# Eight more leaf operands, another leaf order and a searched instruction order in a conditioned block by Strassen products

## The chip, the cores and the metric

The kernel runs on one core of one Trainium2 chip. The metric is the device time in microseconds, median of three runs. The engines are TensorE (PE, with its weight loads as PEld), VectorE (DVE), ScalarE (ACT), GpSimd (POOL) and SyncE (SP, which issues nearly all DMAs). Each works through its own queue in order and waits for the others by semaphores.

## The reference

`x` is (2, 2048, 512) in float32, `cond` (2, 512). The result is `x` after two residual steps:

```python
emb = silu(cond) @ ada_w + ada_b              # six rows of 512 per batch
norm = ln(x) * (1 + scale_msa) + shift_msa
h = gelu(norm @ ssm_w1 + ssm_b1)              # 512 -> 512, exact gelu
x = x + gate_msa * (h @ ssm_w2 + ssm_b2)      # 512 -> 512
norm2 = ln(x) * (1 + scale_mlp) + shift_mlp
hf = gelu(norm2 @ ff_w1 + ff_b1)              # 512 -> 1024, tanh gelu
out = x + gate_mlp * (hf @ ff_w2 + ff_b2)     # 1024 -> 512
```

## The kernel before, in words

**Tiling.** The 4096 rows are cut into 8 blocks of 512 (`TB`); blocks 0 to 3 belong to the first batch row, 4 to 7 to the second (`PER_B` = 4). All matrix products are float32, and a product is issued as two matmul records and two weight loads (two passes).

**Products with seven instead of eight.** Every large product is a 2 x 2 block product done with seven products P1 to P7 of sums of quarters (Strassen in Winograd's form). `first` and `second` (L420, L430) form the sums of the operands, with adds on DVE or POOL; the partial results are gathered in PSUM banks and added out by DVE or copied by ACT. In the ff stage this is done twice over: each of the seven outer products is split into seven inner ones, here called leaves.

**Stages.** First come the modulation rows, then for the eight blocks `ssm1` and `ssm2` in alternation with the norms. Then the ff stage runs four times, `s` = 0 to 3, each for two blocks: `ff1(s)`, then `ff2(s, 0)` and `ff2(s, 1)`.

**`ff1` (L1024).** Seven outer products in the order `OUTER`, each with seven leaves in the order `CARRIED` (L445: P1, P5, P6, P2, P7, P3, P4). A leaf is two products of 256 columns. Two outer products overlap: product n begins at step 7n and does a leaf on every second step (L1099 to L1104). So the seventh (n = 6) shares its first three leaves' time with the sixth, and its last four run alone; in the same way the first product's first leaves run alone. P1, P6, P7 and P4 of one outer product write bank y (one after the other onto the same sums), P2 writes x, P5 and P3 write v (`BANK`, L782). After P1, ACT copies bank y to x; after each other leaf, DVE adds its bank to `hidden`. A leaf that writes a bank must wait until the previous reader of that bank is done. After P4 of some outer products, ACT does the gelus of a finished quarter.

**`ff2` (L1114).** Per block seven outer products of 1024 by 512 by 512 quarters; six of them are split into leaves (128 columns, two products a leaf). The seventh, P6, exists in two forms. With `"P6" in wops` (L1149) it too is split into leaves (`sixth`, L1211): P1, P5, P6 and P7 go through bank 7, ACT copies them to `more`, POOL adds, DVE adds `more` into the bank of P1, and P2, P4 and P3 go into that bank directly. Otherwise `plain_sixth` (L1204) runs eight products of 256 columns straight into it. The weights' leaf operands for P6 are formed by `fw2_sixth` (L934): four sums. Before, it is called for the first batch row at `s` = 1 (L1437), so blocks 0 and 1 take the plain form and blocks 2 to 7 the form by leaves.

**The order of the work.** All instructions are first collected as `Op`s with planned costs (`Plan`, L21). TensorE's order is the order in the program. For the others, `order` (L88) works out how late each may be done, back from the planned start of each TensorE instruction; `simulate` (L111) then goes through time and lets every engine take the most urgent op that is ready. An op with engines "vg" goes to DVE or POOL, whichever takes it. SP's DMA issues are put in order in the same way, with a model of one pipe of 370 bytes per ns. The order found is issued as it stands; on the chip only semaphores hold it. `plan.anchor` (L1394) is the first op of `ssm1(0)`.

Of the kernel before, what the change touches and what calls it, by code (L numbers as in the profile page):

```python
# [1 line left out]

# [12 lines left out]


class Op:
    __slots__ = ("n", "engs", "fn", "cost", "lat", "shared", "size", "lead", "care", "after", "done", "sooner", "deps", "succ", "late", "on", "start", "end", "note")


class Plan:  # L21
# [5 lines left out]


    HOP = 70.0
    ISSUE, FLIGHT, LANDING, RATE, BACKLOG = 640.0, 1300.0, 700.0, 370.0, 4000.0  # L30
    NEAR, SPARE = 30000.0, 1500.0
    RATED, LANDED = 0.5, 4000.0
    LITTLE = 1 << 15
    LANES = 8
    AHEAD, SLACK = 2500.0, 150.0

    def __init__(self, nc):
        self.nc = nc
# [47 lines left out]
        return op  # L86

    def order(self):  # L88
        ops = self.ops
        for op in ops:  # L90
            if op.engs == "p":
                op.deps = {d for d in op.deps if ops[d].engs != "p"}
            for d in op.deps:
                ops[d].succ.append(op.n)
        t, due = 0.0, {}
        for op in ops:
            if op.engs == "p":
                due[op.n] = t
                t += op.cost["p"]
        for _ in range(2):  # L100
            for op in reversed(ops):
                late = due.get(op.n, 1e9)
                for s in op.succ:
                    late = min(late, ops[s].late - (1 + op.care) * (self.HOP + min(op.lat.values()) + op.size / self.RATE))
                op.late = late - op.sooner
            self.simulate()
            wait = ops[self.anchor].start - due[self.anchor]
            due = {n: t + wait for n, t in due.items()}
        return sorted(ops, key=lambda op: (op.start, op.n))

    def simulate(self):  # L111
        ops, hop = self.ops, self.HOP
        left, ready = [len(op.deps) for op in ops], [0.0] * len(ops)
        free = dict.fromkeys("pvags", 0.0)
        self.lock, pipe, holder = 0.0, 0.0, None
        tensor = [op for op in ops if op.engs == "p"]
        at, pools, found = 0, {e: [] for e in "vags"}, {}
        lanes = [0.0] * self.LANES

        def enter(op):  # L120
# [31 lines left out]
        count = len(ops)  # L152
        while count:
# [12 lines left out]
            if op.size > self.LITTLE:  # L166
                pipe = max(start + self.FLIGHT, pipe) + op.size / self.RATE * (1 + self.RATED * op.care)
                op.end = pipe + self.LANDING + self.LANDED * op.care
                found.pop("a", None), found.pop("s", None)
            else:  # L170
                op.end = start + op.lat[e]
                if op.size and e == "s":
                    op.end = max(op.end, pipe + self.LANDING)
            if op.size:
                lanes = lanes[1:] + [op.end]
                found.pop("a", None), found.pop("s", None)
            if e in op.shared:
# [10 lines left out]
            count -= 1  # L188
# [10 lines left out]
def kernel(  # L199
# [824 lines left out]
    def ff1(s):  # L1024
# [28 lines left out]
        QUAD = {"P2": "11", "P5": "22", "P6": "12", "P7": "22", "P3": "12", "P4": "21"}  # L1053

        def leaf(n, j):
            p, f = OUTER[n], CARRIED[j]
            bank = {"y": Y_AT[n], "x": X_AT[n % 2], "v": V_AT[n % 2]}
            t = pair(bank[BANK[f]])
            src = cut(inner[n][f], "p a (c q) -> p c a q", q=G)
            half, at = divmod(FW1_AT[f], 4)  # L1060
            for h in range(2):
                mm(t[:, h, :], slot[n][half][:, at, h * P : (h + 1) * P], src, f in ("P1", "P5") and h == 0, f in ("P2", "P3", "P4"))
            if f == "P1":
                copy(pair(bank["x"]), t)
# [352 lines left out]
    for i in range(1, NBLK):  # L1417
# [8 lines left out]
            norm2(i)  # L1426
        if i == 4:
            ff = weight_fw2(0, 1)
        if i + 1 == PER_B:
            w2_ops = weight2(1, 1)  # L1430
            quarter_row(1)
            w2_leaves[0] = second_leaves(w2_ops)
        if not last:
            hid[i + 2] = ssm1(i + 2, tok[i + 2], w1_ops, second_head(i + 1, hid[i + 1]))
    for s in range(NBLK // 2):
        if s == 1:
            fw2_sixth(*ff)  # L1437
        if 2 * s == PER_B:
            ff = weight_fw2_loaded(1)
            fw2_sixth(*ff)  # L1440
# [58 lines left out]
```

## Time and profile before

| | us |
|---|---|
| median of three runs (566.42 to 566.55) | 566.46 |
| the profiled execution | 566.59 |
| its span, first to last instruction | 564.8 |
| TensorE busy in the span | 557.8 |
| DVE / POOL / ACT busy | 483.1 / 379.0 / 266.0 |
| from P4 of ff1(0)'s last product to that of ff1(1) | 87.32 |
| the same, ff1(1) to ff1(2), and ff1(2) to ff1(3) | 86.66, 86.57 |

The granted TensorE clock is at full speed in every slice. A PE row's busy time overlaps that of the next matmul, so the spacing of matmuls is read from counts in a stretch, and a stall from the idle time of the weight loads (PEld) or from the time between two starts. All adds by DVE and POOL have line L256, all plain matmuls L294, ACT's copies L283 and its activations L274, DMA issues L316: they are told apart by their tiles. `hidden` is the ff hidden state and the ssm hidden state, `turned` the transposed normed rows, `ring` weights and sums of ff1's leaves (and `more`), `fw` the second ff weight and its sums, `near` and `far` operand sums of ff2 and scratch of the norms, `rows` the residual, `marks` statistics.

### The profile page before, as it was taken

What the parts mean: (1) busy time and instruction counts of PE and PEld (TensorE: products, weight loads), DVE (VectorE), ACT (ScalarE), POOL (GpSimd) and SP (SyncE); (2) the same over time, 40 slices, a digit from 0 to 9 for tenths busy, and PEclk for the clock granted to TensorE, in tenths of its full rate; (3) what the DMA queues carried; (4) which work ended last, traced back from release to release, by engine and by line L of the source; (5) the groups of instructions that cost most, each with busy time, mean ns of one, the idle gap of its engine ahead of it and who ended that gap; (6) DMA issues with size and microseconds to landing.
All of it is one profiled execution on the core that took longest, in us unless ns stands there. A gap on an engine that the chain in (4) does not pass through costs nothing.

```text
span 564.8 us, 10322 instructions
## 1 busy us (share of the span) xinstructions
PE 557.8 (99%) x3553; PEld 506.3 (90%) x3553; DVE 483.1 (86%) x918; ACT 266.0 (47%) x534; POOL 379.0 (67%) x514
## 2 busy tenths in 40 slices
PE   8999999999999999999999999999999999999997
PEld 4888889888898988889999889999889999888997
DVE  5696978888879989898989899999999888789776
ACT  3473856674888845557102347212366122336120
POOL 2887638979826687995547866776776784446660
PEclk9999999999999999999999999999999999999999
DMA  8953799989799879895047899078956041820022
GB/s 315 398 221 87 233 343 308 316 240 320 223 268 369 257 271 273 273 323 185 4 147 255 302 286 332 18 204 282 321 172 198 2 151 46 272 95 28 1 75 74
DMA packets 53057, 119.85 MB, mean 212 GB/s; under 512 B 5473, under 2 KB 10509, under 8 KB 51470
## 3 DMA queue, kind: packets, MB, share of 16 engines
q1 hardware_dynamic: 51842, 118.66, 63.9%
q8 instruction: 28, 0.46, 0.3%
q10 hardware_dynamic: 1164, 0.55, 0.3%
q14 instruction: 23, 0.19, 0.1%
HBM read 77.63 MB, written 40.51 MB: 209 GB/s over the span
## 4 chain that ended last, share of the span: by engine, by line
PE 94%; DVE 3%; DMA 1%; issue 1%; POOL 0%; SPq 0%; DVEq 0%
PE bank L294 94%; DMA fw<-in_L_cond_ada_w_dram 1%; DVE hidden L256 1%; DVE near L256 0%; DVE marks L522 0%; PE bank L304 0%; POOL hidden L256 0%; POOL near L256 0%; SPq L316 0%; DVE rows L256 0%; DVE ring L256 0%; DVE fw L256 0%; DVE far L591 0%; DVE turned L656 0%; DVE marks L523 0%
## 5 line engine op out<-in xcount | busy, mean ns | idle before, releaser
L294 PE MATMUL bank<-turned,ring 128*128 128x256 f32 x896 | 208.7, 380 | 0.2 <-DVE turned L656 0.2
L294 PEld LDWEIGHTS bank<-turned,ring 128*128 128x128 f32 x896 | 167.6, 190 | 22.9 <-DVE turned L656 0.5
L256 DVE TENSOR_TENSOR hidden<-bank,hidden 128x512 f32<-128x512 f32 (+1 forms) x171 | 125.2, 755 | 28.0 <-PE bank L294 24.8
L294 PE MATMUL bank<-near,hidden 128*128 128x256 f32 (+1 forms) x470 | 95.3, 350 | 0.3 <-DVE rows L256 0.2
L294 PEld LDWEIGHTS bank<-near,hidden 128*128 128x128 f32 x470 | 82.1, 190 | 10.0 <-DVE rows L256 0.6
L294 PE MATMUL bank<-fw,hidden 128*128 128x128 f32 x640 | 90.4, 275 | 0.0
L256 DVE TENSOR_TENSOR rows<-bank,rows 128x128 f32<-128x128 f32 (+3 forms) x154 | 78.8, 554 | 11.4 <-PE bank L294 10.9
L294 PE MATMUL bank<-ring 128*128 128x256 f32 x336 | 82.4, 381 | 0.5 <-DVE hidden L256 0.5
L294 PEld LDWEIGHTS bank<-fw,hidden 128*128 128x128 f32 x640 | 81.2, 192 | 0.4
L283 ACT COPY bank<-bank 128x512 f32<-128x512 f32 (+2 forms) x88 | 37.3, 425 | 83.3 <-PE bank L294 82.2
L256 POOL TENSOR_TENSOR turned<-turned 128x512 f32<-128x512 f32 (+1 forms) x56 | 63.1, 1139 | 16.7 <-ACT turned L274 9.4
L294 PEld LDWEIGHTS bank<-ring 128*128 128x128 f32 x336 | 63.2, 190 | 11.2 <-issue 1.7
L294 PE MATMUL bank<-fw,far 128*128 128x128 f32 (+2 forms) x644 | 67.6, 278 | 0.7 <-DMA fw<-in_L_cond_ada_w_dram 0.7
L294 PEld LDWEIGHTS bank<-fw,far 128*128 128x128 f32 (+1 forms) x644 | 60.9, 167 | 2.7 <-issue 1.7
L274 ACT ACTIVATE hidden<-hidden,cols 128x512 f32<-128x512 f32 (+1 forms) x66 | 45.0, 712 | 37.9 <-DVE hidden L256 37.8
L294 PE MATMUL bank<-fw,near 128*128 128x128 f32 (+1 forms) x452 | 61.1, 279 | 0.0
L256 POOL TENSOR_TENSOR hidden<-hidden 128x128 f32<-128x128 f32 (+2 forms) x52 | 43.6, 847 | 22.6 <-DVE hidden L256 6.4
L294 PEld LDWEIGHTS bank<-fw,near 128*128 128x128 f32 x452 | 56.0, 192 | 0.4
L256 POOL TENSOR_TENSOR fw<-fw 128x256 f32<-128x256 f32 (+1 forms) x52 | 45.0, 875 | 13.3 <-DVE fw L256 7.7
L274 ACT ACTIVATE turned<-turned,mod,mod 128x512 f32<-128x512 f32 x56 | 41.5, 805 | 8.2 <-DMA turned<-turned 7.2
L256 POOL TENSOR_TENSOR ring<-turned,ring 128x256 f32<-128x256 f32 x37 | 27.8, 757 | 15.8 <-PE bank L294 9.7
L256 DVE TENSOR_TENSOR hidden<-hidden 128x512 f32<-128x512 f32 (+2 forms) x58 | 34.9, 621 | 1.2 <-ACT hidden L274 0.8
(136 smaller groups left out, 692.4 us busy)
## 6 DMA issues: line engine op xcount, KB each, us to landing
ring<-fw_parts SPq DMA_DIRECT2D x28, 512.0 KB
turned<-far SPq DMA_DIRECT2D x52, 256.0 KB
ring<-fw_parts SPq DMA_DIRECT2D x28, 384.0 KB
rows<-x SPq DMA_DIRECT2D x32, 256.0 KB
turned<-turned SPq DMA_DIRECT2D x32, 256.0 KB
out_dram<-rows SPq DMA_DIRECT2D x28, 256.0 KB
fw_parts<-fw SPq DMA_DIRECT2D x21, 256.0 KB
fw<-in_L_cond_ada_w_dram SPq DMA_DIRECT2D x5, 1024.0 KB
```

The lines of the kernel that those rows point to most:

```text
L256: lambda E: E.tensor_tensor(o, a, b, f),
L274: lambda E: E.activation(o, a, func, bias=bias, scale=scale),
L283: plan.add("a", lambda E: E.copy(o, a), [o], [a], {"a": cost}, {"a": cost + 60})
L294: lambda E: E.matmul(o, lhsT, rhs, start=start, stop=stop, skip_group_check=True, **kw),
```

## The change

Three things change.

1. `fw2_sixth` for the first batch row is called right behind `weight_fw2(0, 1)` (in the loop over blocks, `i` = 4) and no longer at `s` = 1. With that `"P6" in wops` holds in `ff2` of blocks 0 and 1 too.
2. The seventh outer product of `ff1` takes its leaves in the order `ALONE`: P1, P6, P5, P7, P2, P3, P4.
3. `order` makes plans with varied urgencies. It starts from the plan that the old rule gives, looks for places where TensorE waits in a plan, follows such a wait back to an op that caused it, makes this op more urgent (or an op that stood in its way less), and plans again, 600 times. A plan's cost is the end of TensorE's last op, as `follow` works it out with the order held fixed, as a mean over four cases (DMA landing 0.7 or 2.2 us, or 1.2 us with the pipe at 0.85 of its rate; DVE, ACT and POOL 3% slower in one). Waits are looked for only behind `anchor`. The cheapest plan is kept. `WAKE` lets the modelled DMA pipe start at 2.2 us in place of 0.

```diff
+    WAKE = 2200.0
...
+    ROUNDS, WARMTH, LEAST = 600, 300.0, 30.0
+    CASES = ((700.0, 1.0, 1.0), (2200.0, 1.0, 1.0), (1200.0, 0.85, 1.0), (700.0, 1.0, 1.03))
...
     def order(self):
...
+            op.ahead = (1 + op.care) * (self.HOP + min(op.lat.values()) + op.size / self.RATE)
+        self.draw_up({})
+        wait = ops[self.anchor].start - ops[self.anchor].due
+        for op in tensor:
+            op.due += wait
+        draw = random.Random(1)
+        wanted, (cost, gaps) = {}, self.draw_up({})
+        best = cost, wanted
+        for n in range(self.ROUNDS):
+            other = dict(wanted)
+            if other and draw.random() < 0.3:
+                del other[draw.choice(list(other))]
+            for d, over in draw.choices(gaps, [g[0] for g in gaps])[0][1]:
+                more = over * draw.choice((0.5, 1.0, 1.5, 3.0))
+                for _ in range(draw.choice((1, 1, 2, 3, 4, 6, 9))):
+                    sooner, rival = d, ops[d].before
...
+                        if draw.random() < 0.5:
+                            sooner, more = rival, -more
+                            break
...
+                other[sooner] = other.get(sooner, 0.0) + more
+            found = self.draw_up(other)
+            if found[0] <= cost + draw.random() * self.WARMTH * (1 - n / self.ROUNDS):
+                wanted, (cost, gaps) = other, found
+                if cost < best[0]:
+                    best = cost, wanted
+        self.draw_up(best[1])
         return sorted(ops, key=lambda op: (op.start, op.n))
+
+    def draw_up(self, wanted):
+        ops = self.ops
+        for op in reversed(ops):
+            late = min([ops[s].late for s in op.succ], default=1e9) - op.ahead
+            op.late = (op.due if op.engs == "p" and op.due < late else late) - op.sooner - wanted.get(op.n, 0.0)
+        self.simulate()
...
+        for case in self.CASES:
+            cost += self.follow(*case, gaps) / len(self.CASES)
+        return cost, gaps
+
+    def follow(self, landing, pace, longer, gaps):
...
+            if e == "p" and start > free[e] + self.LEAST and op.n > self.anchor:
+                gaps.append((start - free[e], [(d, end[d] + hop - free[e]) for d in op.deps if end[d] + hop > free[e]]))
+            free[e] = start + last
+        return free["p"]
...
-        self.lock, pipe, holder = 0.0, 0.0, None
+        self.lock, pipe, holder = 0.0, self.WAKE, None
...
     CARRIED = ("P1", "P5", "P6", "P2", "P7", "P3", "P4")
+    ALONE = ("P1", "P6", "P5", "P7", "P2", "P3", "P4")
...
         def leaf(n, j):
-            p, f = OUTER[n], CARRIED[j]
+            p, f = OUTER[n], (CARRIED, ALONE)[n == 6][j]
...
         if i == 4:
             ff = weight_fw2(0, 1)
+            fw2_sixth(*ff)
...
     for s in range(NBLK // 2):
-        if s == 1:
-            fw2_sixth(*ff)
         if 2 * s == PER_B:
```

More of the change, by code (lines that the diff above doesn't have):

```diff
@@ L1 @@
+import random
 from contextlib import ExitStack
@@ L17 @@
 class Op:
-    __slots__ = ("n", "engs", "fn", "cost", "lat", "shared", "size", "lead", "care", "after", "done", "sooner", "deps", "succ", "late", "on", "start", "end", "note")
+    __slots__ = ("n", "engs", "fn", "cost", "lat", "shared", "size", "lead", "care", "after", "done", "sooner", "deps", "succ", "ahead", "before", "due", "late", "on", "start", "end", "note")
 class Plan:
     HOP = 70.0
+    WAKE = 2200.0
     ISSUE, FLIGHT, LANDING, RATE, BACKLOG = 640.0, 1300.0, 700.0, 370.0, 4000.0
@@ L94, in order @@
                 ops[d].succ.append(op.n)
-        t, due = 0.0, {}
+        tensor = [op for op in ops if op.engs == "p"]
+        t = 0.0
+        for op in tensor:
+            op.due, t = t, t + op.cost["p"]
         for op in ops:
[L97 to L108, printed above, removed]
@@ L109, in order @@
-        return sorted(ops, key=lambda op: (op.start, op.n))
+            op.ahead = (1 + op.care) * (self.HOP + min(op.lat.values()) + op.size / self.RATE)
+        self.draw_up({})
+        wait = ops[self.anchor].start - ops[self.anchor].due
+        for op in tensor:
+            op.due += wait
[10 more added lines that the diff above has]
+                    sooner, rival = d, ops[d].before
+                    held = [u for u in ops[d].deps if ops[u].engs != "p"]
+                    last = max(held, key=lambda u: ops[u].end, default=None)
+                    if rival is not None and (last is None or ops[rival].start + ops[rival].cost[ops[rival].on] > ops[last].end):
+                        if draw.random() < 0.5:
+                            sooner, more = rival, -more
+                            break
+                        last = rival
+                    if last is None:
+                        break
+                    d = last
+                other[sooner] = other.get(sooner, 0.0) + more
[4 more added lines that the diff above has]
+                    best = cost, wanted
@@ new lines, in order @@
+        self.draw_up(best[1])
+        return sorted(ops, key=lambda op: (op.start, op.n))
+    def draw_up(self, wanted):
[4 more added lines that the diff above has]
+        self.simulate()
+        last = dict.fromkeys("pvags")
+        for op in self.sequence:
+            op.before, last[op.on] = last[op.on], op.n
+        cost, gaps = 0.0, []
+        for case in self.CASES:
+            cost += self.follow(*case, gaps) / len(self.CASES)
+        return cost, gaps
@@ new lines, in follow @@
+    def follow(self, landing, pace, longer, gaps):
+        ops, hop, end = self.ops, self.HOP, [0.0] * len(self.ops)
+        free = dict.fromkeys("pvags", 0.0)
+        pipe, lock, lanes = self.WAKE, 0.0, [0.0] * self.LANES
+        for op in self.sequence:
+            e, ready = op.on, 0.0
+            last = longer * op.cost[e] if e in "vag" and not op.size else op.cost[e]
+            for d in op.deps:
+                t = end[d] if ops[d].on == e and not ops[d].size else end[d] + hop
+                if t > ready:
+                    ready = t
+            start = max(free[e], ready)
+            if op.size:
+                start = max(start, lanes[0])
+                pipe = max(start + self.FLIGHT, pipe) + op.size / (self.RATE * pace)
+                end[op.n] = (pipe if op.size > self.LITTLE else start + op.lat[e]) + landing
+                lanes = lanes[1:] + [end[op.n]]
+            else:
+                if e in op.shared:
+                    start = max(start, lock)
+                    lock = start + last
+                end[op.n] = start + last + op.lat[e] - op.cost[e]
+            if e == "p" and start > free[e] + self.LEAST and op.n > self.anchor:
+                gaps.append((start - free[e], [(d, end[d] + hop - free[e]) for d in op.deps if end[d] + hop > free[e]]))
+            free[e] = start + last
+        return free["p"]
@@ L151, in simulate @@
                 enter(op)
-        count = len(ops)
-        while count:
+        self.sequence = []
+        while len(self.sequence) < len(ops):
             best = None
@@ L187, in simulate @@
                     found.pop(x, None)
-            count -= 1
+            self.sequence.append(op)
             for s in op.succ:
```

## The prediction

> **What bounds the kernel now.** I read the page first, then the chain of work that ended last in order of time, then busy time by stage, then what TensorE's weight loads (PEld) waited for. The page:
>
> ```profile
> span 564.8 us, 10322 instructions
> PE 557.8 (99%) x3553; PEld 506.3 (90%) x3553; DVE 483.1 (86%) x918; ACT 266.0 (47%) x534; POOL 379.0 (67%) x514
> PE 94%; DVE 3%; DMA 1%; issue 1%; POOL 0%; SPq 0%; DVEq 0%
> ```
>
> TensorE is busy for 99% of the span and is 94% of the chain. A gain is therefore either fewer TensorE cycles or one of the few stalls between them. The chain shows where those lie:
>
> ```profile
> 2.12 8.43 DMA fw<-in_L_cond_ada_w_dram
> ...
> 33.12 3.72 PE bank L294 x16
> ...
> 206.94 0.59 DVE far L591
> 207.54 0.59 DVE rows L256
> ...
> 208.17 42.65 PE bank L294 x196
> ...
> 254.53 0.69 DVE hidden L256
> ...
> 255.36 82.77 PE bank L294 x544
> ...
> 342.68 86.65 PE bank L294 x588
> ...
> 429.34 86.56 PE bank L294 x588
> ...
> 560.91 0.42 DVE rows L256
> ```
>
> Until 10.6 us TensorE waits for weights from DMA; from 560.9 us only an add, a store and its landing are left (3.9 us of span). Between them the breaks in "PE bank" are short and mostly DVE's. Four of them, 255.36, 342.68, 429.34 and 515.91 us, are one place: ff1's last leaf, P4 of the seventh outer product, once in each of the four stages. Here are the weight loads at those four places, then the P6 leaf of the first outer product in each ff1 (three of the four name ACT as releaser), then the breaks at 208 and 33 us:
>
> ```profile
> 255.33 0.73 PEld L294 LDWEIGHTS bank<-ring 128*128 128x128 f32 x4 [0.61 <-POOL near L256]
> 342.65 0.73 PEld L294 LDWEIGHTS bank<-ring 128*128 128x128 f32 x4 [0.61 <-issue]
> 429.31 0.73 PEld L294 LDWEIGHTS bank<-ring 128*128 128x128 f32 x4 [0.38 <-issue]
> 515.88 0.73 PEld L294 LDWEIGHTS bank<-ring 128*128 128x128 f32 x4 [0.38 <-issue]
> ...
> 215.14 0.51 PEld L294 LDWEIGHTS bank<-ring 128*128 128x128 f32 x3 [0.20 <-ACT bank L283]
> 302.45 0.73 PEld L294 LDWEIGHTS bank<-ring 128*128 128x128 f32 x4 [0.24 <-ACT bank L283]
> 389.33 0.73 PEld L294 LDWEIGHTS bank<-ring 128*128 128x128 f32 x4 [0.24 <-ACT bank L283]
> 475.90 0.51 PEld L294 LDWEIGHTS bank<-ring 128*128 128x128 f32 x3 [0.30 <-issue]
> ...
> 208.17 0.51 PEld L294 LDWEIGHTS bank<-near,hidden 128*128 128x128 f32 x3 [0.64 <-DVE rows L256]
> 33.12 0.51 PEld L294 LDWEIGHTS bank<-near,hidden 128*128 128x128 f32 x3 [0.28 <-POOL near L256]
> ```
>
> The bracket is how long the weight loader stood idle. What TensorE lost is less, because a load normally runs ahead. The matmuls give the rate of exchange:
>
> ```profile
> 253.01 2.11 PE L294 MATMUL bank<-turned,ring 128*128 128x256 f32 x9
> 255.36 1.10 PE L294 MATMUL bank<-ring 128*128 128x256 f32 x4 [0.24 <-DVE hidden L256]
> 256.30 0.61 PE L294 MATMUL bank<-fw,hidden 128*128 128x128 f32 x4
> ...
> 275.00:293.00 18.00, 18.00 (x163) 1.00 0.36 117
> 217.00:241.00 24.00, 24.00 (x113) 1.00 0.91 295
> ```
>
> The last two rows are TensorE alone in a stretch of 128-wide and in one of 256-wide matmuls: one every 18.00/163 = 0.110 us and every 24.00/113 = 0.212 us (a record or two too many at the edges, so up to 2% low; I use 0.111 and 0.216). Nine matmuls from 253.01 us would let the next start at 253.01 + 9 x 0.216 = 254.95; it started at 255.36, and four took 0.94 instead of 0.86. So 0.48 us was lost where the loader idled 0.61, and I subtract 0.13 everywhere: 0.48, 0.48, 0.25, 0.25 at the four ends, 1.46 in all; 0.07, 0.11, 0.11, 0.17 at the four P6 rows; 0.51 at 208 us.
>
> **Part 1, P6 of the ff residual by leaves in blocks 0 and 1.** Now a block without leaves runs 8 products of 256 columns, each two matmul records (two passes), so 16 x 0.216 = 3.46 us. By leaves it is 7 leaves x 2 = 14 products of 128 columns: 28 x 0.111 = 3.11 us. The saving is 0.35 a block, 0.70 for two. The trace has the same comparison made already, since blocks 2 to 7 are by leaves:
>
> ```profile
> core 0: us, PE busy (x) PEld busy (x) DVE busy (x) ACT busy (x) POOL busy (x), PEclk, DMA share, GB/s
> 208.17:255.36 47.19, 46.95 (x216) 40.90 (x217) 42.21 (x69) 26.10 (x42) 42.83 (x61) 1.00 0.87 278
> 255.36:342.68 87.32, 87.08 (x565) 80.68 (x565) 79.13 (x141) 28.95 (x59) 57.07 (x60) 1.00 0.60 204
> 342.68:429.34 86.66, 86.65 (x588) 80.84 (x589) 81.64 (x144) 34.89 (x73) 61.86 (x68) 1.00 0.64 209
> ```
>
> From P4 to P4, the stretch with blocks 0 and 1 takes 87.32 us for 565 matmuls, that with blocks 2 and 3 86.66 for 588. Both hold about the same stalls, so I take the measured 0.66.
>
> Added around it per block: 4 copies on ACT, 2 adds on DVE into the bank, 2 on POOL, 3 operand sums on DVE or POOL; no DMA. Four sums of weights (`fw2_sixth`) move from the start of ff1(1) to weight_fw2, ahead of ff1(0), and pass everything that POOL and DVE have queued in between. Their prices:
>
> ```profile
> L283 ACT COPY ring<-bank 128x128 f32<-128x128 f32 x8 | 1.9, 271 | 6.0 <-PE bank L294 5.9
> L256 DVE TENSOR_TENSOR bank<-bank,ring 128x256 f32<-128x256 f32 x4 | 1.7, 433 | 0.4
> L256 POOL TENSOR_TENSOR ring<-ring 128x128 f32<-128x128 f32 x4 | 2.5, 615 | 2.9 <-DVE turned L256 1.1 <-DVE ring L256 0.8 <-DVE far L256 0.7
> L256 POOL TENSOR_TENSOR fw<-fw 128x256 f32<-128x256 f32 x4 | 2.8, 728 | 0.1
> ```
>
> ACT gets 8 x 0.27 = 2.2 us, DVE 4 x 0.43 = 1.7, POOL 2.5 and, at worst, 6 x 0.73 = 4.4 of sums. What hides them is the stretch itself: with blocks 2 and 3 it carries 81.64 of DVE and 61.86 of POOL without a stall of its own, and with blocks 0 and 1 only 79.13 and 57.07. The tight place is ff1(0), where DVE has 5.0 us free (47.19 - 42.21) and POOL 4.4. Into it or ahead of it must go the four weight sums and block 0's three, 7 x 0.73 = 5.1 us on POOL alone, less if DVE takes some. They fit in 9.4 us; I charge nothing, and 2.4 us if they don't (rivals). Part 1: -0.66.
>
> **Part 2, ff1's last product in the order P1, P6, P5, P7, P2, P3, P4.** Of the seventh product the last four leaves run with no other product between. Now they are P2, P7, P3, P4. P7 and P4 share one bank, so P4 waits until DVE has added P7 out, with one leaf (4 x 0.216 = 0.86 us) as cover; that is the 1.46 us above. New: P7, P2, P3, P4, two leaves of cover, 1.73 us. The first stall needed 0.86 + 0.48 = 1.34, so 1.73 covers it unless DVE is late by another 0.39. I take all of it as gone.
>
> What is late next: P6 now comes one leaf after P1, where three were between. P1 is copied by ACT out of the bank that P6 writes. The same spacing (P1, one leaf, P6) exists at the start of every ff1, where the first product runs alone; those are the four P6 rows, 0.07 to 0.17 us, 0.46 in all. I charge that, since the copy has the same size. The end of the range is a copy that waits behind a gelu:
>
> ```profile
> 247.59 0.72 ACT L274 ACTIVATE hidden<-hidden,cols 128x512 f32<-128x512 f32 x1 [0.46 <-DVE hidden L256]
> 248.25 0.57 ACT L283 COPY bank<-bank 128x512 f32<-128x512 f32 x1
> ```
>
> Here the copy follows directly on a gelu of the fifth product, of which there are four to be done about then. One gelu too many ahead of it costs up to 0.72 at each of four places, +2.9. No instruction is added, and no DMA moves: the weights of all seven leaves are loaded before the product begins. Part 2: -1.46 + 0.46 = -1.00, between -1.46 and +1.9.
>
> **Part 3, the order from 600 plans.** TensorE's own order is the program's; the search only re-sorts DVE, ACT, POOL and the DMA issues and decides who takes a sum. So it can win only stalls. Beside part 2 those that an order could cure are 208.17 us (0.51: a residual add that stands in DVE's queue behind a transpose of the next norm, "far L591" in the chain) and 33.12 us (0.28 at most). It can't cure the minimum latency of P1 to P6, nor the DMA before 10.6 us. Between 0 and -0.8, I take half, -0.4. The loss is bounded by what the present order shows at its worst, two new stalls of 0.5, +1.0. The `WAKE` of 2.2 us only tells the planner when first loads land; it adds no wait on the chip, and it shifts all due times alike, so I charge nothing. The tail is not in the search's cost, which ends with TensorE; I charge 0, at most one add's 0.42.
>
> **The sum.** -0.66 - 1.00 - 0.4 = -2.1 against the profiled execution's 566.59 us gives 564.5; the median of runs, 566.46, lies 0.1 below, so 564.4 us.
>
> **A rule that speaks against part 1.** The trace's 0.111 us for 128 columns is just over half of 0.216 for 256. The Trainium skill, "TensorE: Matmul & The Clock Gate", section "Back-to-back issue gap", says that in a stream of weight loads and matmuls the spacing is set by both, about 81 ns at 128 columns and 131 at 512. Interpolated to 98 ns at 256 (an estimate from that page), 56 narrow matmuls against 32 wide ones would cost 56 x 0.081 - 32 x 0.098 = +1.4 us instead of -0.66, and the sum would be about 566.4. The trace doesn't agree: its narrow stretch is at half the wide spacing.
>
> **The rivals.**
> (a) The new wait for ACT takes the place of the old one: at about half a gelu each, 4 x 0.36 = 1.4 more than charged, 565.8; at a whole one 567.3. For it: ACT has four gelus of the fifth product just there. Against it: in the row above the copy had to let only one gelu pass, although nothing pressed it. 0.10, counted as same.
> (b) ff1(0) is too full: the seven sums pile up on POOL and 5.1 us of them are still ahead of block 0's P6 leaf when it is reached. That is three quadrants x 8 x 0.111 = 2.7 us after ff2(0) begins, so TensorE waits 2.4 us; net +0.3, 566.8. For it: 91% of POOL and 89% of DVE are busy there. Against it: 9.4 us free. 0.06, same.
> (c) Slower: the new order lets a load pass one that TensorE waits for, in the stretch where DMA is full:
>
> ```profile
> 14.07:35.00 20.93, 20.89 (x129) 17.91 (x130) 15.55 (x31) 12.39 (x24) 18.59 (x23) 1.00 1.04 398
> ```
>
> At 398 GB/s each 1 MB costs 2.6 us. It decides (0.2% above before, 1.1 us) once 3.2 us slip, 1.3 MB; two loads of 1 MB give +5.2 - 2.1, 569.6. Against it: loads go out by due time and the first ones are due first. 0.07.
> (d) Narrow matmuls are bound by their weight loads (190 ns each by the page's groups):
>
> ```profile
> L294 PEld LDWEIGHTS bank<-turned,ring 128*128 128x128 f32 x896 | 167.6, 190 | 22.9 <-DVE turned L656 0.5
> ```
>
> Then 56 x 0.190 - 32 x 0.216 = +3.7, net +2.3, 568.8. The x163 row nearly excludes it. 0.02. (The Trainium skill's rule above is this mechanism.) Other new stalls that the search doesn't see, over 3.2 us: 0.03.
> (e) The search returns a plan in which nothing moved: part 3 is 0, 564.8, inside the forecast.
>
> **How the numbers follow.** A measurement of this kernel (three runs within 0.13 us) tells 0.2%, 1.1 us, from no change. The forecast (with e) has 0.72, its own range 563.3 (-0.66 - 1.46 - 0.8, and a little for smaller stalls) to 565.3. Same, (a) and (b): 0.16. Slower, (c), (d) and the rest: 0.12. The range goes up to 566.2, into the middle of (a) and (b), and leaves out some 0.18.
>
> **What would show it.** Right: the stretch from ff1(0)'s P4 to ff1(1)'s P4 has 588 matmuls like the next; no idle of 0.38 to 0.61 before P4; a small wait for "ACT bank" before P6 of the seventh product; nothing of 0.64 near 208 us. Wrong: idle weight loads at that P6 over 0.4 (a), at the first P6 leaf of block 0 (b), or a first ssm1 matmul much after 14.07 us (c).

## The result, and the profile after

| | us |
|---|---|
| before, median of 22 runs beside it (566.37 to 567.08) | 566.52 |
| after, median of 22 runs (567.01 to 568.0) | 567.65 |
| ratio after / before, 95% interval | 1.0018 [1.0012, 1.0025] |
| the profiled execution of after, its span | 567.82, 566.0 |

The kernel became 1.13 us slower. The predicted 564.4 us and the range up to 566.2 both miss. The page of the changed kernel:

```profile
span 566.0 us, 10417 instructions
PE 558.4 (99%) x3577; PEld 507.1 (90%) x3577; DVE 483.7 (85%) x929; ACT 267.1 (47%) x542; POOL 376.1 (66%) x519
PE 35%; DVE 1%; issue 0%; DVEq 0%
```

TensorE is still busy for 99% of the span. The chain's share fell to 35% because it is followed back only to 358 us; I don't use it. What helps is the busy time by stage, cut at the same instructions in both kernels: the first ssm1 matmul, then the first `turned,ring` matmul of each of the four ff1, then the end. First before, then after (columns: stretch, its length, TensorE busy and its matmuls, weight loads, DVE, ACT, POOL, granted clock, DMA share, GB/s):

```profile
14.07:213.45 199.38, 199.10 (x1132) 176.59 (x1133) 165.35 (x341) 134.49 (x269) 145.04 (x243) 1.00 0.84 275
213.45:300.72 87.27, 87.03 (x565) 80.67 (x564) 78.92 (x148) 35.67 (x66) 61.98 (x76) 1.00 0.62 202
300.72:387.60 86.88, 86.64 (x591) 80.93 (x589) 79.56 (x138) 31.82 (x67) 62.39 (x66) 1.00 0.72 238
387.60:474.11 86.51, 86.50 (x591) 80.83 (x589) 80.63 (x143) 32.08 (x67) 63.58 (x68) 1.00 0.49 161
474.11:564.77 90.66, 86.75 (x590) 80.82 (x588) 70.84 (x125) 26.63 (x59) 42.98 (x49) 1.00 0.29 92
```

```profile
15.25:214.12 198.87, 198.83 (x1133) 176.66 (x1133) 164.58 (x341) 134.26 (x268) 143.54 (x243) 1.00 0.82 272
214.12:302.01 87.89, 87.32 (x589) 81.14 (x588) 81.85 (x157) 37.04 (x75) 61.80 (x79) 1.00 0.63 204
302.01:389.11 87.10, 86.76 (x591) 81.00 (x590) 79.34 (x139) 31.81 (x67) 63.95 (x68) 1.00 0.72 234
389.11:475.48 86.37, 86.37 (x591) 80.85 (x589) 79.67 (x144) 32.19 (x67) 60.58 (x68) 1.00 0.50 164
475.48:565.96 90.48, 86.56 (x590) 80.84 (x588) 70.58 (x125) 26.42 (x59) 42.66 (x49) 1.00 0.28 92
```

Read the lengths against each other, row by row: up to the first ssm1 matmul +1.18 (15.25 against 14.07), the ssm stages -0.51, then +0.62, +0.22, -0.14 and -0.18. They add up to +1.19, which is the difference of the spans. So there are two losses, one at the very start and one in the first two ff stages; the second figure is what is left after real gains.

**The gains came.** In ff1's seventh product, P4 no longer waits, and the new wait stands at P6. Weight loads of after, at P6 and at P4 of ff1(0):

```profile
249.60 0.73 PEld L366 LDWEIGHTS bank<-ring 128*128 128x128 f32 x4 [0.26 <-issue]
...
255.53 0.84 PEld L366 LDWEIGHTS bank<-ring 128*128 128x128 f32 x4
```

The 0.26 of idle loader is 0.127 us of TensorE by the times between matmul starts, and the same 0.127 appears at all four places: 0.51 together, where 0.46 was forecast. The stall of 0.51 at 208 us is gone too (the -0.51 above). And the stretch 214.12:302.01 now has 589 matmuls like its neighbours: part 1's leaves are in.

**The loss in the ff stage.** These are new breaks, none of which before has (matmuls, then weight loads):

```profile
258.74 0.71 PE L366 MATMUL bank<-fw,hidden 128*128 128x128 f32 x4 [0.18 <-ACT bank L355]
282.25 0.49 PE L366 MATMUL bank<-fw,far 128*128 128x128 f32 x2 [0.37 <-DVE far L328]
365.66 0.60 PE L366 MATMUL bank<-fw,hidden 128*128 128x128 f32 x3 [0.34 <-DVE rows L328]
```

```profile
277.78 0.41 PEld L366 LDWEIGHTS bank<-fw,hidden 128*128 128x128 f32 x3 [0.20 <-DVE rows L328]
281.18 0.52 PEld L366 LDWEIGHTS bank<-fw,hidden 128*128 128x128 f32 x4 [0.20 <-POOL hidden L328]
```

By the starts of the matmuls (nominal spacing 0.112 at 128 columns) they cost 0.45, 0.63, 0.61, 0.28 and 0.27, with a small one of 0.11 at 368.78: 2.35 us. Check of the first stage: -0.66 (part 1), -0.48 (P4), +0.13 (P6), +1.63 (four of the new stalls) = +0.62, as measured.

**The loss at the start.** DVE in before, then in after; L522 and L595 are the statistics of the first rows of `x`, L1354 and L1427 the copy of `cols`, which waits for TensorE's transpose of the small bias rows:

```profile
4.68 0.69 DVE L522 BATCH_NORM_STATS2 marks<-far 128x6 f32<-128x512 f32 x1 [2.60 <-DMA far<-in_x_dram]
...
5.51 0.66 DVE L522 BATCH_NORM_STATS2 marks<-far 128x6 f32<-128x512 f32 x1
6.33 0.69 DVE L522 BATCH_NORM_STATS2 marks<-far 128x6 f32<-128x512 f32 x1 [0.17 <-DMA far<-in_x_dram]
...
7.57 0.20 DVE L1354 COPY cols<-bank 128x44 f32<-128x44 f32 x1 [0.32 <-PE bank L304]
7.68 0.68 DVE L522 BATCH_NORM_STATS2 marks<-far 128x6 f32<-128x512 f32 x1
```

```profile
4.76 0.69 DVE L595 BATCH_NORM_STATS2 marks<-far 128x6 f32<-128x512 f32 x1 [2.68 <-DMA far<-in_x_dram]
...
8.20 0.20 DVE L1427 COPY cols<-bank 128x44 f32<-128x44 f32 x1 [2.53 <-PE bank L376]
8.32 1.28 DVE L595 BATCH_NORM_STATS2 marks<-far 128x6 f32<-128x512 f32 x2
...
9.78 0.69 DVE L595 BATCH_NORM_STATS2 marks<-far 128x6 f32<-128x512 f32 x1
```

Before, three of the four statistics are done before the copy. After, the copy stands ahead of three of them and DVE idles 2.53 us for the transpose, though the rows of `x` are there (before started on them at 5.51). The last statistics come at 9.78 in place of 7.68. The theory formed from this: with `WAKE` the planner believes that `x` lands 2.2 us later, so it puts the copy first; that costs the 1.1 us. For the ff stage the theory was: the leaf work of part 1 is more than DVE and POOL can do ahead of the second block. It doesn't cover the 0.45 at 258.74, which waits for a copy in ACT's queue, nor the 0.61 at 365.66, which is in a later block.

### The profile page after: what moved, and what is told of

The parts are those of the page before. It is cut to its first block, busy times and chain, and to the rows that moved or that the text cites. A ratio compares the mean times of both kernels' runs of the same rounds, so it can differ in the third digit from the quotient of the medians.

```text
span 566.0 us, 10417 instructions
## 1 busy us (share of the span) xinstructions
PE 558.4 (99%) x3577; PEld 507.1 (90%) x3577; DVE 483.7 (85%) x929; ACT 267.1 (47%) x542; POOL 376.1 (66%) x519
## 5 line engine op out<-in xcount | busy, mean ns | idle before, releaser
L328 POOL TENSOR_TENSOR turned<-turned 128x512 f32<-128x512 f32 (+1 forms) x61 | 67.3, 1116 | 20.6 <-ACT turned L346 9.7
L366 PE MATMUL bank<-fw,far 128*128 128x128 f32 (+1 forms) x656 | 67.5, 275 | 0.5 <-DVE far L328 0.4
L366 PE MATMUL bank<-fw,near 128*128 128x128 f32 x464 | 61.0, 275 | 0.0
L328 POOL TENSOR_TENSOR fw<-fw 128x256 f32<-128x256 f32 (+1 forms) x48 | 42.2, 889 | 15.0 <-DVE fw L328 13.9
L328 POOL TENSOR_TENSOR ring<-turned,ring 128x256 f32<-128x256 f32 x39 | 29.0, 753 | 11.9 <-PE bank L366 8.2
```

The lines of the kernel that those rows point to most:

```text
L328: lambda E: E.tensor_tensor(o, a, b, f),
L366: lambda E: E.matmul(o, lhsT, rhs, start=start, stop=stop, skip_group_check=True, **kw),
```

## The experiments

Fourteen kernels were run. Each gives its median and its ratio to before with the 95% interval; before stayed between 566.52 and 566.54 beside all of them.

### The start

**wake_only.** Before, with nothing but the late pipe:

```diff
-        self.lock, pipe, holder = 0.0, 0.0, None
+        self.lock, pipe, holder = 0.0, 2200.0, None
```

> The kernel before with the modelled DMA pipe starting at 2.2 us and nothing else; only DVE's order at the start differs: the copy of the transposed rows (cols) stands ahead of the statistics of the second to fourth slot. Theory S (the start is lost there): DVE sits idle about 2.5 us before that copy, the first ssm1 matmul comes at about 15.2 instead of 14.1 us, the time is 567.6 (567.0 to 568.0). Rival R (the later start of the changed kernel is chance, or comes from its loads): 566.5 and a first ssm1 matmul at 14.1.

567.18 us (566.82 to 567.83), 1.0011 [1.0002, 1.0019]. Only DVE's order differs from before, and it differs in this one place (the rows are of wake_only):

```profile
7.30 0.20 DVE L1354 COPY cols<-bank 128x44 f32<-128x44 f32 x1 [1.58 <-PE bank L304]
7.42 1.28 DVE L522 BATCH_NORM_STATS2 marks<-far 128x6 f32<-128x512 f32 x2
```

In this profiled run, at the low end (566.82), the copy came at 7.30 and ssm1 started at 14.35. In after the copy came at 8.20 and ssm1 at 15.25: both times 7.05 us later. With the copy behind the statistics, as in before, copies between 7.13 and 8.14 all gave a start between 13.98 and 14.25. So the copy's time reaches the end only when it stands first. By the medians the late pipe costs 0.65 us here (567.18 against 566.53), and the runs spread over 1.0 us as those of the changed kernel do.

**after_moved.** The changed kernel, with four statistics operations issued ahead of the copy, everything else as it is:

```diff
+    todo = plan.order()
+    at = todo.index(plan.copy_of_cols)
+    early = [op for op in todo[at + 1 :] if op.on == "v"][:4]
+    todo = todo[:at] + early + [op for op in todo[at:] if op not in early]
```

> The changed kernel, instruction for instruction, but with four statistics instructions of DVE issued ahead of the copy of cols at the start, as before. Theory S: first ssm1 matmul back at 14.1 us, 1.2 less than the changed kernel, 566.4; the rest of the trace is as in the changed kernel, with about 2.3 us of stalls in ff2. Rival R: 567.6, no change.

566.63 us (566.58 to 566.79), 1.0001 [0.9992, 1.001]; ssm1 started at 14.10, and the five ff stalls stood as in after, at 257 to 281 and 364 us. Four instructions moved past one copy give back 1.02 of the 1.13 us. The spread went as well: after's runs spread over 1.0 us, these over 0.2.

**search_nowake.** The changed kernel with `WAKE` at 0:

```diff
-    WAKE = 2200.0
+    WAKE = 0.0
```

> The changed kernel with the modelled pipe starting at 0 as before: parts 1 and 2 and the search. The start is that of before (14.1 us). The search draws other plans, so the later part may differ: theory W (part 1's work crowds ff2 of blocks 0 and 1, and the search can only half repair it) 566 to 567 with stalls of 1 to 2 us in sum in ff2; rival N (the stalls are luck of one plan) under 565.3 with none over 0.3.

566.62 us (566.57 to 566.84), 1.0001 [0.9993, 1.001]. Behind the start the search ended in the same plan: by the traces, DVE, ACT and POOL run their operations in the order of after but for the copy and one small operation beside it, and the stalls in the ff stage are 0.45, 0.29, 0.28, 0.63 and 0.60. So the late pipe cost 1.03 us at the start and bought nothing there.

**after_early_turn.** The theory was that the transpose comes late because it stands behind the warm-up matmuls (products of an identity tile that TensorE does first). It was put behind the second of them:

```diff
+    todo.remove(plan.turn_of_rows)
+    warmed = [op for op in todo if op.engs == "p"][1]
+    needs = [warmed] + plan.ops[:5]
+    todo.insert(max(todo.index(op) for op in needs) + 1, plan.turn_of_rows)
```

> The changed kernel with one TensorE instruction moved: the transpose of the loaded rows, on which DVE's copy of cols waits, is issued behind the second warm-up matmul and not behind the fourth. Theory H (DVE waits there for TensorE's warm-up, whose length hangs on when the clock is granted): the copy of cols at about 5 us in place of 8.2, first ssm1 matmul at about 14.1, 566.5 and within 0.2 us over the runs. Rival L (the copy waits for its small loads to land): the copy at 7.5 us or later, 567.5, spread as in the changed kernel.

569.38 us (567.3 to 571.12), 1.0046 [1.003, 1.0062]: that theory fell, for the copy of `cols` still came at 7.93. The rival had the copy's time, but not the 569.38. TensorE in this run:

```profile
7.59 0.31 PE L376 MATMUL bank<-far,fw 44*128 44x44 f32 x1 [2.46 <-DMA fw<-in_L_cond_ssm_b_dram]
7.83 5.90 PE L366 MATMUL bank<-far 128*128 128x512 f32 x8
```

In this execution the small rows landed only at about 7.5 us, so TensorE idled 2.46 us in place of DVE. The eight warm-up matmuls behind it took 5.90 us, 0.74 each, where four took 1.35 (0.34 each) behind the transpose in after_moved: TensorE worked at about half that rate, and ssm1 started at 18.15. So the warm-up isn't all that the copy waits for; the rows' landing is the other part, and it varies (the last section has more).

### Part 1

**p1_only.** Before with the call moved, under the planner of before:

```diff
             ff = weight_fw2(0, 1)
+            fw2_sixth(*ff)
...
-        if s == 1:
-            fw2_sixth(*ff)
```

> The kernel before with P6 by leaves in blocks 0 and 1 alone, ordered by the old planner. Theory N (the new stalls in ff2 come from the searched order): no stall of 0.3 or more in ff2 of blocks 0 and 1; 566.5 - 0.7 = 565.8. Rival W (they come from the added work of part 1): the stalls at block 0's and block 1's start, about 1.6 us, are there too, 566.5 - 0.7 + 1.6 = 567.4.

569.22 us (569.02 to 569.78), 1.0047 [1.0034, 1.0059]. Part 1 alone makes the kernel 2.7 us slower in place of 0.66 faster.

**sums_only.** The same move, but blocks 0 and 1 keep the plain form. It reads a weight quarter that one of the sums has by then replaced, so the rows of blocks 0 and 1 differ from the reference; the amount of work is the point.

```diff
-        by_leaves = "P6" in wops
+        by_leaves = i > 1
```

> The kernel before with the four weight sums ahead of ff1(0), as part 1 has them, but blocks 0 and 1 still take the plain form of P6 (it reads a weight quarter that one of the sums has by then replaced, so the rows of blocks 0 and 1 come out otherwise than in the reference). If the moved sums are what is too much (part 1 alone gave 569.22, with 2.14 us of stall at 278.5): the stall stays, 568.5 us or more. If it is the leaves' own sums and adds: no stall over 0.5 us near 278 us and the time of before, 566.5 to 566.8.

566.62 us (566.53 to 567.43), 1.0005 [0.9996, 1.0014]: the four moved sums cost nothing. The leaves do. The stretch of ff2(0) in before:

```profile
256.25:278.50 22.25, 22.25 (x185) 21.81 (x185) 19.73 (x44) 9.05 (x19) 10.79 (x12) 1.00 0.25 86
```

In sums_only:

```profile
256.25:278.50 22.25, 22.25 (x186) 21.81 (x185) 20.68 (x42) 9.54 (x20) 11.64 (x12) 1.00 0.27 92
```

In p1_only:

```profile
256.25:278.50 22.25, 22.25 (x200) 22.22 (x200) 21.11 (x42) 10.35 (x24) 12.46 (x15) 1.00 0.29 93
```

At its end, TensorE, DVE and POOL in p1_only:

```profile
280.78 1.94 PE L294 MATMUL bank<-fw,far 128*128 128x128 f32 x12 [1.98 <-POOL far L256]
...
275.69 5.20 DVE L256 TENSOR_TENSOR rows<-bank,rows 128x256 f32<-128x256 f32 x9 [0.19 <-PE bank L294]
...
277.55 2.50 POOL L256 TENSOR_TENSOR far<-hidden,far 128x512 f32<-128x512 f32 x2
280.00 0.72 POOL L256 TENSOR_TENSOR far<-hidden 128x256 f32<-128x256 f32 x1
```

DVE at the same place in sums_only:

```profile
275.34 0.68 DVE L256 TENSOR_TENSOR far<-far 128x512 f32<-128x512 f32 x1
276.07 5.20 DVE L256 TENSOR_TENSOR rows<-bank,rows 128x256 f32<-128x256 f32 x9
```

At about 276 us DVE begins a run of nine residual adds, 5.20 us long. In sums_only the second block's operand sums (`far`) on DVE are done by then. In p1_only, which has the adds of the first block's leaves besides, some of them are not: they are left to POOL at 1.25 us each where DVE takes 0.68, and TensorE idles until the sum begun at 280.00 is there: 2.14 us, then 0.33, 0.17 and 0.55. Every kernel has a plan of its own, so these rows show what is late, and not which added instruction pushed it back. DVE was already busy for 19.73 of these 22.25 us in before. But a full DVE alone makes no stall: from 255.00 to 278.00 us in p2_port (below) it is busy for 22.12 of 23.00 us, and no stall there is longer than 0.32. By these rows it is the sums still to be done when the residual adds begin.

**blk0_leaves.** Leaves in block 0, not in block 1. Block 1's plain form again reads the replaced quarter, so its rows differ from the reference.

```diff
-        by_leaves = "P6" in wops
+        by_leaves = i != 1
```

> The kernel before with P6 by leaves in block 0 but not in block 1, by the old planner. p1_only waited over 3 us at block 1's start for operand sums. Theory D (block 1's P6 leaf comes first in the block and wants its sums and everything queued ahead of them early): that wait goes, 566.5 - 0.33 = 566.2. Rival A (the work added in block 0 alone fills DVE and POOL): at least 1.5 us of stall stays at block 1's start, 568.

571.06 us (570.43 to 571.35), 1.0076 [1.0064, 1.0088]. The stall stays, 2.13 us, without any leaf of block 1: so it is the first block's leaf work that makes the second block late, not the second block's own. Why it is even slower than p1_only is taken up in the last section and stays open in part.

**p12_old.** Parts 1 and 2 (the diffs of p1_only and p2_only together), under the planner of before.

> Parts 1 and 2 ordered by the planner of before, without the search and the late first loads. Part 1 alone gave 569.22 (stalls of 2.14, 0.33, 0.17 and 0.55 us at the second block's start), part 2 alone 566.25 (0.28 under before). If parts add up: 568.9 us, and the search is then worth 2.3 us against 566.62. If part 1's loss comes from that one plan rather than from the work: under 567.5 us.

569.29 us (569.09 to 569.75), 1.0046 [1.0033, 1.0059]. Against search_nowake the search is worth 2.67 us. It works, but mostly by repairing what part 1 breaks under the old order.

**p12_port.** Parts 1 and 2 with the search, `WAKE` 0, and POOL held to the planned order (the edit of p2_port below).

> Parts 1 and 2 with the search, without the late first loads (566.62 without the port order), and POOL held in the planned order as in the run before. If the stalls of 0.45, 0.28, 0.27 and 0.63 us between 257 and 281 us come from clashes of VectorE and POOL, at least two of them go and the time is about 565.5 us. If they come from the sheer sum of work in the second and third product of the feed-forward stage, they stay and the time is 566.6 us.

566.66 us (566.55 to 566.99), 0.9999 [0.9991, 1.0007]. Each engine has its operations in the order of search_nowake, and the stalls stay, 0.28, 0.27, 0.64 and 0.62 among them. So they don't come from POOL running ahead of DVE.

### Part 2 and the search

**p2_only.** Before with the new leaf order.

```diff
-            p, f = OUTER[n], CARRIED[j]
+            p, f = OUTER[n], (CARRIED, ALONE)[n == 6][j]
```

> The kernel before with the order P1, P6, P5, P7, P2, P3, P4 in the seventh product alone, ordered by the old planner. Theory of the prediction's part 2: the four waits before P4 (1.46 us) go, the four waits for the copy before P6 come (0.13 each, 0.5): 565.5. Rival: the old planner puts DVE's adds so that the wait before P4 stays or a gelu stands before the copy: 566.5 to 567.

566.25 us (565.82 to 566.62), 0.9994 [0.9985, 1.0003]. All four waits before P4 are gone. At P6 it lost 0.125, 0.70, 0.22 and 0.125, the 0.70 here:

```profile
336.73 1.10 PE L294 MATMUL bank<-ring 128*128 128x256 f32 x4 [0.46 <-ACT bank L283]
...
335.38 0.72 ACT L274 ACTIVATE hidden<-hidden,cols 128x512 f32<-128x512 f32 x1 [5.35 <-DVE hidden L256]
336.01 0.58 ACT L283 COPY bank<-bank 128x512 f32<-128x512 f32 x1
```

The copy of P1 lies behind a gelu that ACT had just begun: rival (a) of the prediction, once in four. The four losses, 1.17, against the 1.46 that went come to -0.29; the medians give -0.27, which is inside the interval of no change.

**p2_search.** Part 2 and the search, no part 1, `WAKE` 0.

> Part 2 and the search, without part 1 and with the pipe starting at 0. Theory W: without the added work no stall over 0.3 us in ff2, the four waits before P4 gone, 0.5 for P6: 566.5 - 1.46 + 0.5 - 0.4 = 565.1. Rival N (a searched order opens stalls by itself, since its durations are not the chip's): 566 or more, with stalls of 0.3 to 0.6 in ff2.

567.15 us (567.09 to 567.79), 1.0012 [1.0003, 1.002]. Slower than p2_only, by one stall of 1.59 us at 385.20 that isn't in the plan. POOL and DVE, and TensorE behind them:

```profile
383.03 5.15 POOL L328 TENSOR_TENSOR fw<-fw 128x256 f32<-128x256 f32 x6
383.54 0.94 DVE L328 TENSOR_TENSOR fw<-fw 128x256 f32<-128x256 f32 x1
...
386.14 1.94 DVE L328 TENSOR_TENSOR rows<-bank,rows 128x256 f32<-128x256 f32 x4
...
386.81 0.71 PE L366 MATMUL bank<-fw,hidden 128*128 128x128 f32 x4 [1.33 <-DVE rows L328]
```

**p2_hold.** The same kernel, with POOL's first sum made to wait for the DVE add ahead of it in the plan:

```diff
+        if op.n == 2900:
+            op.after = plan.ops[2858]
```

> Part 2 with the search and without the late first loads, as in the run before of that kind (567.15), but the first of POOL's four weight sums ahead of TensorE's stall at 385.20 (1.59 us) is made to wait for the VectorE add that the plan has ahead of it. Theory Q (POOL began its sums about 2 us ahead of the plan because their data landed early, and VectorE's adds beside them took 0.94 us in place of 0.41): the stall of 1.59 us goes, about 565.6 us. Rival (the rows were late for another reason, such as their own inputs): the stall stays within 0.3 us of 1.59 and the time at 567.1.

565.52 us (565.47 to 566.07), 0.9981 [0.9973, 0.999]. The stall is gone and 1.63 us with it:

```profile
383.57 0.41 DVE L328 TENSOR_TENSOR fw<-fw 128x256 f32<-128x256 f32 x1
...
384.58 2.27 DVE L328 TENSOR_TENSOR rows<-bank,rows 128x256 f32<-128x256 f32 x5
...
385.07 1.54 POOL L328 TENSOR_TENSOR fw<-fw 128x256 f32<-128x256 f32 x2 [1.97 <-DVE rows L328]
```

The same DVE add took 0.41 us with POOL waiting and 0.94 with POOL at work, and the residual adds that TensorE needs began at 384.58, not 386.14. The Trainium skill, "SBUF — State Buffer", section "Who interferes with whom", says that a VectorE instruction with two operands in SBUF contends with a GpSimd instruction that reads SBUF. The trace agrees (0.94 beside 0.41). The plan has such a rule as well and puts POOL's first sum behind these DVE adds; on the chip POOL began at 383.03, ahead of them, and nothing held it back. The edit shows that this order was the cause; why POOL could begin so early no run shows.

**p2_port.** The same, for every POOL operation that the plan has behind a DVE operation of that kind, in the planner's rule:

```diff
-                if e == "g" and holder and holder.on == "v" and start > max(free_at, ready[op.n]):
+                if e == "g" and holder and holder.on == "v":
```

> The same kernel, with every POOL operation that the plan puts behind a VectorE operation of the shared kind made to wait for it, not only where the plan foresaw a clash. Theory Q: as above, the stall at 385.20 goes and others of its kind with it, 565.0 to 565.6 us. Rival: the added waits delay POOL's sums by more than the clashes cost, new stalls behind POOL of 0.5 us and more, 567 us or slower.

565.55 us (565.47 to 566.6), 0.9982 [0.9974, 0.999]: the same result by a rule instead of by hand, with the same small stalls (0.32 and 0.33 at 256 and 345 us). These two beat both kernels, by 1.0 and 2.1 us.

**blk1_leaves_port.** p2_port with the leaves in the second block too, the sums between the two blocks' ff2:

```diff
         for blk in range(2):
+            if s == 0 and blk == 1:
+                fw2_sixth(*ff)
             ff2(s, blk, *ff)
```

> Part 2, the search without the late first loads, POOL held in the planned order (565.55 so far), and P6 by leaves in the second block too, with the four weight sums between the two blocks' ff2. If the first block's leaf work is the load that doesn't fit, the second block's leaves save their 0.33 us with no new stall over 0.2: 565.2 us. If the sums or the second block's own leaves are too much for the stretch from 255 to 300 us: stalls of 0.5 us and more there, 566 us or slower.

565.59 us (565.51 to 565.8), 0.9983 [0.9974, 0.9992]. The expected 0.33 is there in its own stage; from ff1(0) to ff1(1), p2_port first:

```profile
212.56:299.99 87.43, 87.38 (x566) 80.82 (x564) 82.88 (x153) 35.99 (x66) 62.36 (x71) 1.00 0.62 204
```

```profile
212.85:299.79 86.94, 86.94 (x577) 80.80 (x576) 83.21 (x152) 36.51 (x71) 63.76 (x79) 1.00 0.64 206
```

Without the first block's leaf work there is no stall of the old size near 278 us (0.23 is the largest). Some 0.1 of the 0.49 gained is the difference to p2_port's stall of 0.32. The 0.49 is lost elsewhere, since the search ended in another plan: 0.29 before ff1(0), 0.29 in the next stage (a stall of 0.36 at 335.32) and 0.29 in the last (one of 0.30 at 474.56). No gain over p2_port was reached.

## Why the prediction was wrong

The forecast was a gain of 2.1 us; 1.13 us were lost. In the traces, where the first to the last instruction should have become 2.06 us shorter and became 1.19 longer, the difference is the 1.18 at the start and the 2.35 of new stalls, less some 0.3 of old stalls cured beyond the forecast. Medians of kernels that differ by one step at a time give the sum as it came out: before 566.52; part 2 alone 566.25 (-0.27, inside its interval of no change); the search with POOL in order 565.55 (-0.70); part 1 on top of it 566.66 (+1.11); without POOL's order 566.62 (-0.04); with `WAKE` 567.65 (+1.03). The price of part 1 depends on this path: under the planner of before it is +2.69 (p1_only), and between the two searched kernels without POOL's order it is -0.53 (p2_search 567.15, search_nowake 566.62), since only p2_search has the stall of 1.59.

- **Part 3, "it shifts all due times alike, so I charge nothing": failed.** It measured +1.03. `WAKE` moves the loads, but not the copy of `cols`: so it isn't a shift of all but a change of order between two of them, and what it put first was an operation that waits. The prediction looked for trouble at the start only in a load that slips (rival (c)). Its sign, a first ssm1 matmul much after 14.07 us, came (15.25), but not its cause: the first rows of `x` came as before (statistics at 4.76 against 4.68 us), and the ssm stages behind were 0.51 us shorter.
- **Part 1, "they fit in 9.4 us; I charge nothing": failed.** The saving of 0.66 was right. The cover was measured in the wrong stretch: I weighed ff1(0), where the seven sums were to go; the moved sums were free (sums_only). The tight place is the end of ff2(0), where the second block's operand sums must be done before DVE's nine residual adds; with leaves in the first block they weren't, under the old order (p1_only, blk0_leaves), and 0.28, 0.27 and 0.63 of stall were left there by the search. That the leaf work of the first block brings the large stall is shown; how it pushes the sums back is read from the rows only. Rival (b) had the kind of failure, work piled up ahead of a block, but the wrong block; that its 2.4 us is near the 2.14 us of the stall is chance. The comparison with blocks 2 and 3 over 87 us hid that, because an average over a stage says nothing of its last 5 us (and that stretch has a stall of 0.21 of its own, at 386.16).
- **Part 3, "-0.4" for the search: the wrong size, and against the wrong baseline.** I gave the search stalls of before to cure. It did cure the 0.51 at 208 us. But it had to cure part 1's stalls first (worth 2.67), left 2.35 of stalls that before doesn't have, and in p2_search added 1.59 that isn't in its plan. The 0.45 at 258.74 comes with the searched order: p1_only and p12_old do the same leaf work without such a stall. ACT begins the copy waited for at 257.21 and 256.83 us there, at 258.33 in after. My bound of "+1.0" for new stalls was too small.
- **Part 2, "-1.46 + 0.46": right in the changed kernel**, -1.46 and +0.51. Alone it kept only 0.27, because the copy met a gelu once.
- **The rule that spoke against part 1** was rightly set aside: the 589 matmuls of the first ff stage came at the usual spacing between their stalls.

What stays open: why the plan has fewer ff stalls than the chip shows in part 1's kernel. The order between DVE and POOL is not it (p12_port); that the planned costs of the adds are too low was not tried.

## What to carry to other kernels

When added work is to be hidden, look at the last microseconds ahead of the place where its results, or those of its neighbours in the queue, are needed, not at the free time of the whole stage. A number in a planner that "only delays loads" still changes which of two operations comes first on an in-order engine; ask which of them waits. And a plan that counts on one engine staying off a shared resource must be enforced by a wait: one here was worth 1.6 us.

## What the runs showed of the hardware

**An add that doubles.** DVE's add of 128x256 from SBUF took 0.41 us alone and 0.94 beside POOL's, whose own rose from 0.73 to 0.86 (5.15 / 6).

**After a wait of 2 us the granted clock can be halved.** blk0_leaves behind its stall (the granted clock is the third number from the end):

```profile
281.15:284.57 3.42, 3.42 (x19) 3.42 (x18) 3.38 (x8) 1.03 (x4) 0.60 (x1) 0.50 0.89 294
```

p1_only behind nearly the same one:

```profile
280.70:284.00 3.30, 2.86 (x19) 2.39 (x20) 3.27 (x7) 1.03 (x4) 1.26 (x2) 1.00 0.72 236
```

TensorE had been idle for 1.97 and 1.98 us. In one kernel 3.42 us at half rate followed, in the other none. The slow stretch holds 1.7 us of lost work, but not all of it is lost time: in the same place p1_only stalls for another 0.33, 0.17 and 0.55 us. It isn't what makes blk0_leaves 1.84 us slower, either: of its five runs, the three with a mean granted clock of 0.999 or 1.0 took 570.43, 570.53 and 571.35 us, and the two with 0.996 took 571.06 and 571.23. What the rest is stays open. The Trainium skill, "TensorE: Matmul & The Clock Gate", section "What's actually happening", tells of a free-running window of about 3.4 us. The length of the slow stretch agrees; here it followed an idle time well below the window.

**Neither the warm-up nor a small load is constant.** The same eight first matmuls took 6.63 us in after and 5.14 in after_moved:

```profile
1.34 6.63 PE L366 MATMUL bank<-far 128*128 128x512 f32 x8 [1.34 <-POOL small L393]
```

```profile
1.34 5.14 PE L366 MATMUL bank<-far 128*128 128x512 f32 x8 [1.34 <-POOL small L393]
```

The small bias rows that the transpose needs vary too. The semaphore that it waits for came at 6.5 us in after_moved, 6.9 in wake_only and 7.6 in after, though the loads are issued in the same order. In wake_only the warm-up was done first, and TensorE stood idle for the rows:

```profile
7.03 0.23 PE L304 MATMUL bank<-far,fw 44*128 44x44 f32 x1 [0.31 <-DMA fw<-in_L_cond_ssm_b_dram]
```

With the copy of `cols` at the head of DVE's queue the later of the two reaches the end of the kernel, which goes with the 1.0 us spread of after's runs; with the statistics ahead of it, it doesn't. How much of that spread each of them makes was not measured.
